# A transformer block on one core: the values' first halves are cast out of PSUM by VectorE instead of ScalarE, with a new order of the work

## The chip, the core and the metric

The kernel runs on one NeuronCore of a Trainium2 chip. Its engines work side by side, each through its own instructions in order: TensorE (PE, matmuls; PEld, its weight loads), VectorE (DVE), ScalarE (ACT), GpSimd (POOL) and SyncE (SP), which issues the DMAs here. The metric is device microseconds for one execution, less being better. The kernel before takes 1051.68 us (median of 3 runs, 1048.98 to 1051.96).

## The reference

The input is x, 8 batches of 512 rows of 512 columns, float32. Cut to what matters:

```python
x = x + layernorm(attention(layernorm(x)))
x = x + layernorm(ffn(layernorm(x)))
# attention: qkv = x @ w_attn + b_attn; 16 heads of 32; a rotation of q and k by head;
#   causal softmax(q k^T) * 512**-0.5 @ v; then @ w_proj + b_proj
# ffn: two layers; each normalises its input, rounds it to 8 bits by the row's largest
#   value, and multiplies by weights rounded to -1, 0, 1 times their mean size;
#   exact gelu between them (512 -> 2048 -> 512)
```

## The kernel before, in words

**Precision.** TensorE multiplies 16-bit floats. Where more is needed, a float32 tile is split in two: a first half, the value rounded to f16, and a remainder, the value minus the first half, also f16. A product then takes three passes (first by first, remainder by first, first by remainder). For the values v the two halves are made out of PSUM at the end of `values` (L538 to L563): the first half by one instruction (L558), the remainder by the next (L560). Both read the same 128x256 float32 piece of an `mm` PSUM tile, and write into one SBUF tile `vt` of 128 x 8 heads x 65 columns: 32 of first halves, a column of ones, 32 of remainders.

**Tiling and streams.** Rows are handled 128 at a time (4 tiles of a batch), heads in groups of 4 (a unit, 128 columns) or in pairs. The work is cut into streams, each a Python generator that yields after every step; a step is a handful of instructions, mostly on one engine. The streams that the text speaks of:

- n, N: load x, normalise it and split it (L491, L496); w, H, J, B, R: load and prepare the attention's weights; t, T, Y: load the feed-forward weights, sum their sizes (L426) and round them (L461)
- Q: queries and keys of a unit (L565; matmuls L575, copies out L587 on ACT and L589 on DVE). V: values of 128 rows and 8 heads (L538): two steps of 6 matmuls (L545), one step with the first half (L558), one with the remainder (L560). There are 64 such pieces
- S: scores (L596; matmuls L610, mask and minimum L624 and L635 on DVE). A: probabilities (L646): exponentials on ACT (L661), a first half on ACT (L667), a remainder on POOL (L669), then DMA transposes `pT<-ph`; 24 steps a unit, 32 units, with transposes in the 12th, 16th, 20th and 24th step. W: the weighted sum of a pair of heads (L682; matmuls L696 of `pT` with `vt`), 7 steps, 64 pairs; the third is the first to read the later transposes
- G, r, P: gather heads, load the residual, project (L741) and add. F, X, Z, C: feed-forward: normalise and quantise (F), expand with Gelu on ACT (X, matmuls L827, Gelu L836; every fifth step), quantise (Z), contract (C, matmuls L883) and store

**The order.** The string `ORDER` (L36 on) holds 4345 letters. The loop at the end of `block_kernel` reads it and takes one step of the named stream for each letter; `pin` (L952) then ties every instruction to the one before it on its engine. So the string fixes the order of the instructions on each engine, the DMA issues on SP included. What it does not fix is time: an engine that waits for another delays what is queued behind.

**Buffers.** PSUM has two `mm` tiles (queries and keys, values, projection, contraction; L120) and three `sc` tiles of two banks (scores, weighted sums, expansion; L119). Matmuls for the next tile of a kind can start only when an older one has been read out.

**Function tables.** ACT loads a function table (ACT_TABLE_LOAD in the trace) when its order goes from an exponential to a Gelu or back.

Of the kernel before, what the change touches and what calls it, by code (L numbers as in the profile page):

```python
# [37 lines left out]
JHJJNNTNRtNtTTtTtTHNNQHQQQQHJnJNtTJHNwYHQYYHYNYQYJQQQHwBYYHQtYYHQJJQHYYQQJSSBTQYYQSQQYYQQHQSSAAQ
AAQVYAAVtVJtYAAAttSSVAQYQAQtQSAAQQQAQJSAAQAABBQQAAAVJSVVAAAQJSAVSVVVVJRVVSAVVVVSAAAVAVnrSVTSQQVA
TVQVAAWNSnQVVQAQWrWWVnWWnQAAAVVTAVQTQQNNNNAWWWWWSWANAWVNNNAAAAAASNNNNNWSSRAATAQAAAASNAWWQNASAANA  # L40
VNVVWWWASGGAAASSWWSWWWWWWAAAAVVVGVAVSVSASNAVVVVAAANAANAWQAAQQQSQSAAAnQGQQGAAWQGSSSQWWWWAAVQAAQVS
WWWWWWWAAVAAAAAQWVAAQRRRRRRQSSAQSSAtWWWQAtASQSQQQAWAQWGGWWWGAVArAWQWQWWWWWASSASAQAVQTQVAATYVQYYY
GGGSSAAAAQQYYYYQQQSQAAAQYAAAPPPPPQPYWPWSSPVPAVPWVVFWWWWPPnAVPASFSFAAAASAAASPVVVAYPYAAAFFQQQQSSQW
WWFWWQWAAAASWAQQAAFAAYQQVSVNNYPSAAANVAVFSYQXAAANNNFAFAAXXXNXNXXAFFXQrnXXGPPFSSNNPPNWGWPVWNNWWAWA
WWVWWWWSPAAAAWVVAAAAVVVASZSYANNNAASFVYVVZArPYYPVAZXWZAAAVFnXXXXXFPXZAAXPXXSSAAAZZZQPGQPQSSWPSQQF
GWZWQQWSWQWAGWAZWWZQWQAWQWCGWZACAQAAQAWSSSAAZAAAQQQQQACAGAAAGASZZCWCWCSAAAVCVVGAAZCSSVQCSCWCWFWQ
WSWQWQAWWWWAAAAACVCWVQQFAAVQSVVZQWVAAASPVVPGQWSZAQQQQFGGNPQAZSSCQAAPQAAQQWWWWNWAAZZXZZVnXWAVANVV
AAAAPSAZXVFFPFZVVPSPNAZZnXASQSWQWWVQWQWAAPWPAZQAAWAQXQQQSQNNCQNSFNXCSAXQAXNnNANAASSFFXPZAXPZZWNr
NANSNNFCWWAWWWCPnGCZGWFPWCPPFWAANWWCZAAANWNWNSPSZZAAAVCVVVCWACAAZACXSCFXVXVXVVPQFSVQSAFFFZVAAAVQ
VZNSFZZXPXAAQQQQXFXQXFAXNQSZPQWPWSPXPWXCCZQWWZZAZZAPCAXFAACQWZPAAZCAPrXCAXZSFZFFZPPCFPSPSCPCXGGC  # L50
XXGWWWWWWGAAXASZZCCACPZWVZANCCCCZrVFCZXSFZVVZWCASQCZWAQAAAAACAQGAAFGSCQQCSCQQWNQWWWZWZZGSAAQCPXA
WQWWWWWWXAPCAAAAACCVSAAQWFZXVVGQVVFSXVSSXVVCrGVZFZXPGVPXSXPFZFFAZAVVQAPQASPAPQAAAAAAAAAWWSQQQQnZ
ZFXXCQCZQAZZCQQCSSCWFWFWWWCAAWWQWWWASCZVWPAVAACWZVSFVQCQnXPZAQFSAXXAZQAAZCZCACCSPASSAPAACASACAZA
XQAAQPXZXPXXPCXPQWWZZFGCZZWQWWQWGXZAZWQXCFAZAXWCWCAWWAWWCPrFNFNXNCQPQVCANAXFZnPFFNXVXNNWSNNAXZZX
ZCCZCSCPNVNCXCPVSSrNZCPnZZZZNCXAXAPZZAZZAFXACAPVNCNNAVSAPSZCXASZCVAVAAAVCZAAZSSAAVVCVSQZPCCASAAA
AXCQCWWSQVCPQVXXWQQWXQWVFVNWQCrPAZQPZZZQPGGGXAPGFZZAQWSQXAQPSCWWAWQWWWACQASNXFACFZZFQCAAASWFCZWW
CAAZAQFQQCGGSXCFQWPWZZZXWWPSAAAAAGAQNFACXACAQAZWSFFFXCSACVWWVnWWWZAAQSQPFXXZZWVXXWAAGVVNXFXSQZAG
FXAQVVSQAGSSZQXXZQCCZVVQZAAAAZQFVQAXSQVVAWFCFFQAZCWZACQAQPCPZXSCSCWPCWPCASXWrAZWZAZZPZZXXZAAAAFA
CWCAAVAACCXCVSnAZSQPPVVrSPPSQCPWWWWWPQPAXAAAQSZZPCAZQFQZZFWCAAZZZSPPQCQCAAAWQFCQCQWCWNNCXWWXWSWG
PAAAAnXQVNGCAFCFFCWWWWWWWNCNNNWAAZVVFXVZAANZZCCNSVAPVSPAVSSVSFrNNAAAAFPAAACPSAAAAANXCNPAXFACXZZn  # L60
CXCXSSXZZNVNZFNCASXAPPCVVZACCAVFFCACCAAXXZZSXSXPFQCCPQrNWWFWAQWPXQXXWXPGGWSZZGQFZZQZZCWWZNXPAAAA
GWPWSAANAAZCZPWWWCAQSCQCQAZAZCQCZSQFAWGQAAZZACQSZQWCCCCQAAWSQQQVXZVSVVQWNWQWPAWQAPVGGQCWAVWWWWWW
XXAnAWSAQQASZSVVXZFGPFXXSQXQGZGCXQFAPAFFAASQASFPZZAAAAQQSAPAFAQAAPZXXQACSAQCSQQQZFFnCSCVWCWVAAZZ
APSWWWWVCFVVrWAWWVCPAZAZZWWAVVVWWAAASFAWnCZZACVCVVSXAAASPZCQFZZZCCXQACAASXAAAQXQQQQSQCSXQWCXCXQN
NXCXCANWCWWCWWZZFSNNNAAACANNAFAAXNNQNNNZQnFFZCVCGCGXWWWXWZWAWWWAFXCCVNFVVVSPNNVPXArZSSSZZAZAVPVS
QNAAAACSAAAAAPZAXXPQXXAQXPPZPPrQQPSQXSPAZQNPPZPZXSQXQFCQXCSAAPXCZZZZSWWCWCWWCAAAAAAFFAZAQAAZQVZC
AVXAZCVVPZAXPXWXPCZCSCFFFXPGGGWWZWPCXWCSWQWFQWFPCAGCAZAQSZSZAWACQZZAQQZCSSFAAACAAAZQNZWPGQCAFrQC
QCSWFQZQZACAVWVVGWWWCVWWWWWVWWCGACAZVAACSWGFVSSVFZVGXVXXVVVGSQXPAAAQPSAAZAVASXXQACrSVVPAQAFQPXFS
AFZAAQAZPXPFQWXZPZQZZNXCPSPPPAAQPQPWnWSWPZnWWQQCPZVCAAWZAAAASAFFFVVnZAVZSCZSCQCQWWQWQCWAWCAASAAA
SAAQQQAAWQCQXQZZNNZXNZCANZZWSXCCNAAACQNCNNCCXASSCWCQVCAZXNNNSCNSNWCWWXCWWCXXAFFAAZAAAGGWWWAWWFNA  # L70
rWNNWSCXAAAXVXWSCCCQXQQFVXZAAZAAQAVSVSSXAZPPFQQFAQSFZZZVAFAAAVXVQXPQXQXPZQQWWPXPZCSCArVPPZXZZZZV
XWWWVVVCVCXAZAXCWPPAZZAPVAVPXCPFZCPFZZZGFGGWSSCPWWWAZCSAAGAZAXPSQSWCQWWZAZZFAQFFFFXCQAXXAAACCWAF
AAACAASCZQCCXXQAZCXZQZACZSrCZQZCQASSWGWCAAWCWWZWACZGXWSCXSQXAAPPZCZCWWWWWWAAAACVAZCSrXZFGAXVQWQX
VXSXAZQCVCSFFFSQAGXPCQCAQCFSFCAZQZQZGZGASQCZAAAAAQCQAWSQQQCXZZFAZZZZAVCXCVVVXWPWAPWAAAAAFPAFWCCP
XPFPXWXVXCPWPFPFXZFZFSXASZCZrZZPVXZPZXPXXAVVACSXAPCSCQZZZZSACWWWWWQCAWAZACAQZFCSPFZPFFFPAFFAXXQW
CCQXQXAZZCCAZZCACWXXCrCZZZPACSWCSZPCPWCSPSCWWCAZZAZPAQAWSQXAZAZFASAAGGWAPPAAFQFXSAPQXCAFFSWWWZXZ
AZAQQPWAPSWWCFCCWPGAAAZAAAAXXPXXSXGAZGPAXAZCFSZZZAPCZSZZVVAFVVAAPAAZZAZACSCCSCGCCCCFAZArWSXZWWWW
WWWWWWWWXWXFSFAFASCASGAACCAPAFFAAAAAAZXAZXXCFXXXXZZZXXXXFCZFFFXZZZCCCGXCXWWCCXCWWWWWWWWWWWWZZGGC
GGZrZZZCXXCCXXZZCPXPZPCPCZPCZPPPCCZZrZFFXXCFFZZZZFXCFZFXCPCCZPCXCXCZZCCPXXZZCPPZPZCPZPFFFXFXPrXP
ZCPCCPPFPPZFZFZPXZZZCFZFXCXXCXXZZZFZCFPCXCCFFPFZCZXXXXZXCPXCCrXPPZZXPPPZZZZXFZZFXCZZFFZZFFFZCXCC  # L80
XCXCXXCZZZZCXXCCCCZCCZCZCXZXZZCCXCXXCXXCZZZZZZZZXZCXXCCZZCXZZXCZZZCZZCCCCCCCCCCZZCCCZZZZZCCZCCCC
# [5 lines left out]
def block_kernel(  # L87
# [450 lines left out]
    def values(b, half, c):  # L538
        xT = xTs[b]
        vt = vts[half * NT + c]  # L540
        ps = mm_tile()
        n = 0
        for hw, hx in PASSES:
            for k in range(NE):
                nc.tensor.matmul(  # L545
                    ps[:, :256],
                    xT[:, c, hx, k, :],
                    wv[hw][:, k, half * 256 : (half + 1) * 256],
                    start=(n == 0),
                    stop=(n == 3 * NE - 1),  # L550
                )
# [6 lines left out]
        nc.scalar.activation(hi, v, AF.Copy, scale=back)  # L558
        yield
        nc.vector.scalar_tensor_tensor(  # L560
            vt[:, :, HD + 1 : 2 * HD + 1], v, back, hi, ALU.mult, ALU.subtract
        )
# [482 lines left out]
```

## Time and profile before

| | |
|---|---|
| median of 3 runs | 1051.68 us (1048.98 to 1051.96) |
| the profiled execution | 1051.51 us |
| its span, first to last instruction | 1049.7 us |
| instructions | 22994 |
| mean granted TensorE clock | 0.978 |
| POOL busy | 759.7 us (72%) |
| DMA, mean | 173 GB/s |
| ACT casts of v, L558 | 64 of 367 to 398 ns, from 64.6 to 906.7 us |
| DVE remainders of v, L560 | 64 of 409 to 425 ns, from 67.4 to 908.1 us |

Times are in microseconds from the span's start. A group of instructions is shown as line, engine, operation, output and inputs, shapes, count, then busy time and the mean of one in ns, then the idle time of that engine just before them and what ended it. A line of the timeline is start, duration, engine, line, operation and count. A row of windows has one engine after another with its busy time and, in brackets, its instructions; after them come the granted TensorE clock (1.00 is full), the mean busy share of the DMA engines (it can pass 1) and GB/s. Matmuls overlap in the pipeline, so PE's busy time and the duration of one matmul overstate what one costs; the distance between starts is the better measure.

### The profile page before, as it was taken

Reading aid. Unit: us, or ns where it says so; the run is one execution under the profiler, and the core shown is the slowest. Engines: PE = TensorE matmul, PEld = TensorE weight load, DVE = VectorE, ACT = ScalarE, POOL = GpSimd, SP = SyncE. Lnnn points to the kernel's source line nnn. Section 1 sums busy time; section 2 is a strip of 40 time slices with the busy share of each in tenths; the row PEclk is TensorE's granted clock in tenths of the full one; section 3 lists DMA queues with packets and bytes.
Section 4 is the critical chain, followed back from the end, with each engine's and each line's share of the span. In section 5 each row is a group of like instructions: output and inputs, shape, how many; then the busy total and the mean of one; then the engine's idle time right before and its main releaser. Section 6 shows DMA issues by size and latency. Waiting matters only on the chain.

```text
span 1049.7 us, 22994 instructions
## 1 busy us (share of the span) xinstructions
PE 977.2 (93%) x8258; PEld 511.0 (49%) x8258; DVE 855.8 (82%) x2674; ACT 904.8 (86%) x1502; POOL 759.7 (72%) x608
## 2 busy tenths in 40 slices
PE   5787888899999999999999999999999999999995
PEld 4544544445555555555545455454454454544442
DVE  7898789989998888887988897888778888866752
ACT  5789998999999998999899999889999889964552
POOL 5249875888877778877888688677967678865544
PEclk9898899999999999999999999999999999999998
DMA  9369998999999988999999999989999879995553
GB/s 308 111 143 205 185 222 128 183 185 194 192 188 181 163 177 163 201 176 183 178 196 177 170 192 178 167 160 192 185 169 175 171 142 170 198 193 110 110 101 80
DMA packets 585027, 181.10 MB, mean 173 GB/s; under 512 B 564304, under 2 KB 568400, under 8 KB 584912
## 3 DMA queue, kind: packets, MB, share of 16 engines
q1 hardware_dynamic: 584912, 179.63, 90.2%
q8 instruction: 64, 1.05, 0.4%
q14 instruction: 51, 0.42, 0.1%
HBM read 29.64 MB, written 8.39 MB: 36 GB/s over the span
## 4 chain that ended last, share of the span: by engine, by line
PE 26%; ACT 25%; DVE 18%; DMA 11%; POOL 10%; issue 9%; SPq 1%; POOLq 0%; ACTq 0%; DVEq 0%
PE sc L827 7%; ACT p L661 6%; PE mm L883 6%; DVE p L624 5%; POOL ph L669 4%; DMA pT<-ph 4%; DMA qT<-q 4%; PE mm L575 4%; ACT ph L667 3%; PE mm L545 2%; PE sc L696 2%; ACT junk L865 2%; ACT h L836 2%; PE mm L741 2%; ACT L836 2%
## 5 line engine op out<-in xcount | busy, mean ns | idle before, releaser
L669 POOL TENSOR_TENSOR ph<-p,ph 128x768 f16<-128x768 f32 (+1 forms) x192 | 355.7, 1856 | 112.8 <-ACT ph L667 92.6
L624 DVE CUSTOM_DVE_ANT_0 p<-sc,mask,e_scale 128x384 f32<-128x384 f32 (+3 forms) x512 | 255.4, 546 | 25.1 <-POOL ph L669 13.2
L883 PE MATMUL mm<-wout,qT 128*128 128x512 fp8e4 x1024 | 260.1, 383 | 6.6 <-ACT row L901 5.1
L827 PE MATMUL sc<-wfc,qT 128*128 128x512 fp8e4 x1024 | 254.6, 379 | 3.9 <-DVE low L624 1.9
L661 ACT ACTIVATE p<-p,nmax 128x384 f32<-128x384 f32 (+3 forms) x512 | 253.5, 552 | 3.0 <-DVE nmax L635 2.5
L575 PE MATMUL mm<-xT,wqk 128*128 128x512 f16 x768 | 203.6, 384 | 2.2 <-DVE vt L560 1.3
L667 ACT CAST ph<-p 128x768 f16<-128x768 f32 (+1 forms) x192 | 172.4, 898 | 5.0 <-DMA pT<-ph 2.0
L827 PEld LDWEIGHTS <-qT 128*128 128x128 f16 x1024 | 96.6, 98 | 117.6 <-issue 9.7
L883 PEld LDWEIGHTS <-qT 128*128 128x128 f16 x1024 | 95.1, 98 | 115.3 <-issue 15.3
L696 PEld LDWEIGHTS <-pT 128*128 128x128 f16 x2560 | 97.1, 98 | 51.6 <-issue 11.9
L575 PEld LDWEIGHTS <-wqk 128*128 128x128 f16 x768 | 70.4, 98 | 83.2 <-issue 16.8
L545 PE MATMUL mm<-wv,xT 128*128 128x256 f16 x768 | 105.1, 278 | 5.8 <-DVE src L589 3.7
L696 PE MATMUL sc<-vt,pT 128*128 128x65 f16 (+1 forms) x2560 | 100.3, 187 | 10.9 <-DMA pT<-ph 4.5
L741 PE MATMUL mm<-wp,oT 128*128 128x512 f16 x384 | 103.2, 381 | 0.8 <-DVE src L589 0.8
L861 POOL TENSOR_SCALAR h<-h,hnm,hqs 128x1024 f32<-128x1024 f32 x64 | 80.1, 1252 | 30.4 <-DVE hnm L857 28.8
L545 PEld LDWEIGHTS <-xT 128*128 128x128 f16 x768 | 73.9, 99 | 37.0 <-issue 11.0
L610 PE MATMUL sc<-src 32*128 32x128 f16 (+3 forms) x1536 | 74.8, 298 | 16.9 <-DVE low L624 9.8
L783 POOL TENSOR_TENSOR q<-h,q 128x1024 f16<-128x1024 f32 x32 | 68.7, 2146 | 24.0 <-ACT q L778 20.1
L865 ACT ACTIVATE junk<-h 128x1024 bf16<-128x1024 f32 x64 | 67.2, 1050 | 16.5 <-DMA qT<-q 12.7
L850 DVE TENSOR_REDUCE htop<-h 128x1 f32<-128x1024 f32 x64 | 76.3, 1211 | 4.6 <-ACT h L836 4.5
L778 ACT CAST q<-h 128x1024 f16<-128x1024 f32 x64 | 66.6, 1040 | 13.2 <-POOL h L861 11.8
L836 ACT ACTIVATE h<-sc,fsc 128x1024 f32<-128x1024 f32 x64 | 71.1, 1111 | 1.9 <-PE sc L827 1.5
(161 smaller groups left out, 1380.8 us busy)
## 6 DMA issues: line engine op xcount, KB each, us to landing
row<-in_x SPq DMA_DIRECT2D x32, 256.0 KB, 3.6
x<-in_x SPq DMA_DIRECT2D x32, 256.0 KB, 3.2
out<-row SPq DMA_DIRECT2D x32, 256.0 KB, 2.7
tw<-in_w_fcT SPq DMA_DIRECT2D x8, 512.0 KB, 8.3
tw<-in_w_outT SPq DMA_DIRECT2D x8, 512.0 KB, 4.4
wraw<-in_w_attn SPq DMA_DIRECT2D x8, 256.0 KB, 4.8
pT<-ph SPq DMA_TRANSPOSE x128, 5.6
qT<-q SPq DMA_TRANSPOSE x96, 4.3
```

Of the source, the lines that this page charges most:

```text
L545: nc.tensor.matmul(ps[:, :256], xT[:, c, hx, k, :], wv[hw][:, k, half * 256 : (half + 1) * 256], start=(n == 0), stop=(n == 3 * NE - 1),)
L575: nc.tensor.matmul(ps, w[:, hw, k, :], xT[:, :, hx, k, :], start=(n == 0), stop=(n == 3 * NE - 1),)
L624: nc.vector.tensor_tensor_reduce(p[:, j, at : at + (i + 1) * P], scs[t][:, j, at : at + (i + 1) * P], mask[:, T - (i + 1) * P :], e_scale[ ...
L661: nc.scalar.activation(pj, pj, AF.Exp, bias=nm[:, i, 2 * t + j : 2 * t + j + 1], scale=-1.0)
L667: nc.scalar.copy(hi, p)
L669: nc.gpsimd.tensor_tensor(lo, p, hi, ALU.subtract)
L696: nc.tensor.matmul(oo[:, j, i, :width], probs[u, PARTS[i]][:, half, j, STARTS[i] + c, :], vt[c][:, h, :width], start=(n == 0), stop=(n == ...
L741: nc.tensor.matmul(ps, oTs[b, k][:, ho, i, :], wp[hw][:, k, :], start=(n == 0), stop=(n == 3 * NE - 1),)
L827: nc.tensor.matmul(ps[:, o1, :], xsT[0][:, n // NE, n % NE, :], wfc[:, n % NE, ts(o, 512)], start=(n == 0), stop=(n == 2 * NE - 1),)
L836: nc.scalar.activation(h[:, ts(o2, 1024)], ps.rearrange("p a f -> p (a f)"), AF.Gelu, scale=xsc, accum_out=hsum[:, o2 : o2 + 1],)
L865: nc.scalar.activation(junk, hh, AF.Square, accum_out=hsq[:, o2 : o2 + 1])
L883: nc.tensor.matmul(ps, hT[0][:, half, k, :], wout[:, o2 * NF // 2 + k, :], start=(n == 0), stop=(n == 2 * NF - 1),)
```

## The change

Of `values`, one line changes; of the order, all but the last line of letters is new:

```diff
         v = ps[:, :256].rearrange("p (h d) -> p h d", d=HD)
         hi = vt[:, :, 0:HD]
         back = 1.0 / (X_S * V_S)
-        nc.scalar.activation(hi, v, AF.Copy, scale=back)
+        nc.vector.tensor_scalar(hi, v, back, None, ALU.mult)
         yield
         nc.vector.scalar_tensor_tensor(
             vt[:, :, HD + 1 : 2 * HD + 1], v, back, hi, ALU.mult, ALU.subtract
```

```diff
 ORDER = """
-nNNNwHIwHHHNwJJNJNNnNHJBBBBBBBBBNNNNRHJJwRRRNNBNBnNHHHNNHHRwJJtHJNNJHRBtnNwwJNJtRHHBBRNNHRNNTJTH
...
+nNwHwHwHJNNNNJBNNtHJnHTJnwNBNBBBBBNBBRHNJRNNRRtBtHNTJHwwNNNHRHHJwJJJnBNHHwNNBNJBRNRJtNtHJHRNwNJB
...
```

Both strings have the same number of letters of each kind. Letters stand at other places throughout, mostly by a few positions: the first t moves from the 63rd letter to the 18th, the first T from the 93rd to the 23rd, I from the 7th to the 154th, the first S from the 171st to the 176th, the first W from the 295th to the 296th, the first X from the 716th to the 725th. The first half's instruction now stands on DVE's queue, after what the order puts before it there; ACT's queue no longer holds it.

More of the change, by code (lines that the diff above doesn't have):

```diff
@@ L36 @@
 ORDER = """
-nNNNwHIwHHHNwJJNJNNnNHJBBBBBBBBBNNNNRHJJwRRRNNBNBnNHHHNNHHRwJJtHJNNJHRBtnNwwJNJtRHHBBRNNHRNNTJTH
[L38 to L81, printed above, removed]
+nNwHwHwHJNNNNJBNNtHJnHTJnwNBNBBBBBNBBRHNJRNNRRtBtHNTJHwwNNNHRHHJwJJJnBNHHwNNBNJBRNRJtNtHJHRNwNJB
+HHHJJNRJRTTHJNNNNNNHnNTJtNtTQtQTTYHHHHQQYQYHYnJNYYtJJYYnJIBYYQQQQQQHHQYYJHQYQTQSSHSYQAQQQYYQQQSS
@@ new lines @@
+QBAAQAYYAAtVAVAAVYVAAASSQQQSQQQSAVAJVAAVJQAVQASAQQAAVStVtQQSABBVAVVVVStVNVSVVJtAArJAAAAAAVTVAAAV
+RAVSSQQWQQVVVWWnWWASAQQQVAVWAQnVTQQTVNNNTNWNNNSSSWNWWWWWWAAAAAAAANNNNSAVSSWATVQWVRAANAASNSNWNNQA
+AAWWWSAAnAAGGWAAASSSVWWWWWAAAGAWVVVSVQQAVNVAAAAWANAASSAAASAQQVVVWASAVGAWRWGSRWAWGAASQAQAQWWQWQWW
+QWWAWAAAAAVQQVQAAARSRRWQVRQVQGSASASSQQrQWQWQWWWWGWAASAAWtWQWWtWNWWSAASAGVVVQAQATTYYVYYSGASGAGAAA
+AAAQYYSAQQQQQQQAYQAYASQPQQYPPWYWPAPYVVVPPSSPPWVPWWAWAWFAASAAPVVArAPSFPWVFSVWWQQAQAASAAAFWQQQFYFW
+QWQSASQWVPAPAQAASVNFNSYAnnPAYAASFVAANAAAQSVAYANNFFNNXGXXAXAAXXXXWAWWWXXWPWPGWQFNANNNNNPPSPSVVWFF
@@ new lines @@
+WWWWWVSAAVAVAVYSASAAAPPVFSAAVYVVYNNZNZYZVAWAAVAAXAXXPAPAAXXPAXPXZrAZPPFXFSSZSXZQQQGZWWWWWFWXGGWQ
+AGQASQQZASSQAQAAWWWWQACWZZQWQWZAACAASSZZSGZZAAAAAGQGCQACSQWQAQAAAAAQZSAACCVWVVSAAVCCCSSQCCSWWWQW
+ZWPAAQFAAWQCWVWVnWWAQWAQAFAVAVAWSVFSQVQVQVGWSACQQZPQNQGGWQSAQnVAQAWWAFPAAASQWVQNXZPWASVPXWFPAXPC
+VSQAPSZAAAVNAQWVWWQAZSZWWNWQVAZZZAZZFAVCXAPAQWQnSrQPFXCSQAXQACQNNXXFNSAFSCNZPNAANQNnQSXNCAWWWWPW
+WPFCPFFAAACAXNPNNNSNGZGWWrCSWWWPVWnZAAAASANWXNAZNAAVAACXXCVVQXPCPZZFWSZFZQZAACAVACAXXQXVVVSXSVQV
+XWWAAZPQVVPQFFQCAZrPFFZFQAFPAWWPXQSWSAPCZPQCFSXAPFQCXPXFQZPZZZXCWAASCZPCAAAAAXSPZFCFFZSZGPZGCGWF
@@ new lines @@
+WXAWWAPVWXVXZAWWAACCAAACZZZSCQCCXZVVCQWZZCWAAQXZZZSQASCWACQQFQGAGPAPCSQCQSWWWZWCZQAAZCSXGWWWWWWF
+XWGNrAAAAAASAXAAACQACAQVAXCACCVWSFVZQVXVQXAGQSSSPQVFFZASGVAXXQNVQVPANCVXnZGPWZVWPVCAAASXNPAWWSCW
+WPZCASQZACAZZQCWAWWWWQWAWAPAZQXZSCXXWPAZFAAQQAAZrAASCXZVCSSCZZZVVASVXXQXQFPFXAAACAACCCPQSPQPFFWA
+PFXFFFSZZAZAQQFQWQPWQCCQNCWCWCXnWANZXZZAZCPPNGXXGZWQAAZCXNCZAWZNCANNQFXFCZSSrNnNZWFnVZNWVCCCPCNC
+ZZWWWWVVXFPXXAXAPASCPNZZZCSZAPXZZCXPCrVSAANNASAAXVCSFVAVCXVZZZNCANAASAAASAZAAPPVZVVZCCCSSQAXAQAC
+WQAPASAAAWACQVCQQWWrWXVXQWXVVPQPQNZFCZPZZQZGGPZGFAXAWSQQAPXCQGSWWAWAQWWWACSAQAXZZCQWWACZFAFWQSQC
@@ new lines @@
+QFCFGFQNSZCAAAXCQFWWWWZZSXXAAACGWSCCGQXZPAFAAZAAAACFSWVWVPWZZAWWWFFSAFQZXQVZVWAXVXPNXSQXZFSGQVXA
+ASXCQVFGCAXZAAQQVXVZSGQQAVQZFZSXVAVQACFFAAQCZWWZCNAAFQQZPCFSAPCAWWPCXSSACPCAPXWZZZZWAZnZnZXXAACC
+AAAAAAWVCSZXVCVSQPPVSSrPCPAAAXAQPWWWWZZPQZCWPPQrAAQZSACFQZZWWFCQAPPACSAAZFSZQCQCQNNCXQFFCWACXXWP
+WWNAGAQNGZNCNNNWWWWWVWAACWCWWVWVXAFAnFnACCAZCrSZNAZVVPVSPSASAANAZVAVPNCSAPAASFNAFNACAAAXXCXXFPCX
+XPNXNNCSCVAAZZSZSCVCZVFXAAACCXZSXPAAAVFQCCAZFZSSPPQPQXXQPGZGNQZXACrGFCXWXWFFFWZZZZQPPZWWWGWWAWCW
+WWXWCAQACNZSCAQCQCZZSZQAAAAACSZZAWAAANQQAACCGCZACCACQWPQSQSWGQCVNQXZQVSQVWQZVWPWQVWWWWQVGPWWWWXX
@@ new lines @@
+WSAAAAAVXZAZZQQSSPFAGXGVGXSQXFFQFrFAAASAAXAQAPAFZQPSASQPQQFPXAQCQSCQCAWWAAAAAAZSXZQCSCZZQVWWVWFP
+WCFAZSVFnVWWFVWWWWWVPAXCAAZZVVVAWCSVSCVVXQXQXZAAAQAAPnnAZAAAZZCCZZCCSSACAZAAFAQQQQXSSQCQCXWAQANC
+NXNCWXNCZXFNCAAWNCANAWWNSAFFFAAXXWCNnNNZGFNGNZZQQVCWWWWWWWXVXCAZNCCWNSPVVVXPNVSZSSCVVPrQAAAPSCZP
+ZAAAAAZAAAAAASZNXXQXXQXPPPPAXQFPSPQQZZZZFSFXQPXXQPCQZSZCSZAAPQCNXAAAAASWWZCWWCAQQVACAVAZAZACArSX
+XWAZZCWZZZVVPPPXXFACCFPFCFXPGGGWWWWWCPGXSWQCWFAAFZZFQPCSCQSZAZCWQACAAAQSCAAAAZAQQWQNCZQCQFQZSZSC
+ZQWZCCVPrNZWGGGAVVVCACWWWFAWWWWWWVWWCVVVVSSAAASAVXVVVXXSVQZXCrCAFPGASAnFFGGPVAQVAAAZFXAXAPASQXQP
@@ new lines @@
+SPAFAAFXQZPSZXZZnQAPSPPPPQPWWQXAPQWWPQZWZAAAWSZPCZQQAZVWFFSFCAVVAAnVCZZZSSCQACAFWQWQWQCWASWAACAA
+AAQSQQZCQZWZAQXQAANNNAXNWZCSNCCAZZASACQANXCCCXCNZQWSNCWVCXZSCWWFANNCNSXCAXWAACAAWNNGrSXGWWAWAWAW
+WWNNANCACAAWXXXCCZVSQVXQZSSAXQAQVXSFAFAAAVQQZFPZSQPZZVCFVVAPQAFAArXXQXFCQPQQXPWPVWPAVZSFZPVVXCVW
+WCWCWZZZZZXXVZXCZZPPAAPVAAVPXPCAZZZFZAAFXPZGGGWSSZSAACPWCWWWWWPAXSQFZFCAZZQSFXFAAAAFCCQXXQAACSAA
+AAACGCCCWFZQQZXZXGZACSAZZASAZCQGCWSQCQCXCWWWWWZWCAAAAAAACCXSAQXSWWZGZCPZCAQXWPWWWZCSXXZVXXWFQFVC
+XVSAQVGACZQrCSSQAXAFZCQAFQPCFZSFAQCQWQWCGQSCQCXZZZAAAAAAFSZQQGVZZXVZCAVVACCrXAWPZAAWPWPWPAFAPACA
@@ new lines @@
+FPFXFZXPZXPPZZZVWXCXFCFSSPXAXAAVPXZPZZVZVSPXZZZZXZZCSQCAQCQAPCQCrSWWPWAWWAASFFAXFFFZFAAQPCFFQZWW
+XACXCCCZZXXCCAACWXZXZZAGZAPWCCSPSCZPSCPZPZZCSrAAAWAWWZSGAWWAAAAAAAFFQCZQCSAQSQQCFXQPFAACPXSPPXZS
+WAACWZWWWAAWZZAAAAZPFXXCFFAXPGWXGAGCAPXPSXXZSZZVZVCVAZSZSAZCAACVASPGrZAAZAZZACPCCCFCFZWWWWWCWWWC
+WWAWXWWXWSXFCSXFSFGPASFAAAAAAAAACCGZFAXZAFAAZXXXCXXXXFCZZZZCXFZFZCFCCWCCWCXXXXGWWWWZXWWWWWWWWZGC
+GXXZZGCCCrCZZXZZZZZXPCCXPPPPPPCrPZZZFFFFCXFXZZZZFZFCCCPZCXCCXCXCCPCXXXZPXZCCZZZPPPZPZCCPFFFFPXPZ
+CPCrPPFPZFFPZPXZZZCXZFZZXCFXPXCXXZZCPZFCXCCCFXFXFPFXZZXXZPCCCrXPZXCZCXPCPPXFZZZZZZXFFFZZZZFFFCZX
@@ L82 @@
+XCCXXXCZCCCCZZZZCZCXXZCZZCCXXZZZZZCCXCXXCZXXCXXXCXXCCCZZZCZZCCCCZZZZZZZCZCCCCCZZZCCCCCCZZZZZCCCC
 CCCCCCCCCCCCCCCCCCCCCCCCC
```

## The prediction

> **What bounds the kernel now.** I read the busy shares first, then the matmuls' own spacing, then busy time by stage, then the waits of the two engines that the edit touches. The first part of the page:
>
> ```profile
> PE 977.2 (93%) x8258; PEld 511.0 (49%) x8258; DVE 855.8 (82%) x2674; ACT 904.8 (86%) x1502; POOL 759.7 (72%) x608
> ```
>
> No engine is the bound by these shares alone: PE is busiest, ACT is 49 us ahead of DVE. Busy PE time is pipelined, so the timeline of PE in a dense stretch gives the real price of a matmul:
>
> ```profile
> 605.72 1.02 PE L883 MATMUL mm<-wout,qT 128*128 128x512 fp8e4 x4
> 606.58 0.82 PE L545 MATMUL mm<-wv,xT 128*128 128x256 f16 x6
> 607.24 0.49 PE L696 MATMUL sc<-vt,pT 128*128 128x65 f16 x12
> 607.57 0.60 PE L545 MATMUL mm<-wv,xT 128*128 128x256 f16 x4
> ```
>
> From start to start, 4 matmuls of 512 columns take 0.86 us (216 ns each), 6 of 256 take 0.66 (110 ns), 12 small ones of L696 0.33 (27.5 ns). Starts of L610's groups lie some 40 ns a matmul apart. The groups of PE between 250 and 900 us hold 2237 matmuls of 512 columns (483 us), 492 of L545 (54), 1754 of L696 (48) and 1044 of L610 (42): 627 of 650 us. So the middle is a dense stream of matmuls, with at most 23 us to win. Busy time by stage:
>
> ```profile
> core 0: us, PE busy (x) PEld busy (x) DVE busy (x) ACT busy (x) POOL busy (x), PEclk, DMA share, GB/s
> 60.00:80.00 20.00, 17.11 (x140) 10.21 (x138) 19.44 (x63) 16.09 (x30) 11.46 (x7) 0.91 0.57 91
> 80.00:150.00 70.00, 55.25 (x681) 33.66 (x683) 56.89 (x202) 66.13 (x121) 60.34 (x45) 0.88 1.09 206
> 150.00:210.00 60.00, 51.82 (x494) 28.04 (x486) 56.26 (x180) 53.19 (x93) 42.65 (x33) 0.97 0.91 160
> ...
> 250.00:900.00 650.00, 641.19 (x5527) 329.11 (x5525) 549.38 (x1711) 609.53 (x990) 505.82 (x394) 1.00 0.97 178
> 900.00:1050.00 150.00, 133.20 (x758) 61.56 (x756) 86.37 (x230) 82.17 (x132) 81.72 (x70) 0.96 0.64 128
> ```
>
> The reader is to see three regimes. Up to about 240 us PE is starved, and DVE is the fullest engine at 60 to 80 (97%) and 150 to 210 (94%), ACT at 80 to 150 (94%). In the middle PE is full and ACT is at 94%. From 900 on the matmuls of the feed-forward part remain. The chain of waits between 130 and 210 us is mostly DVE (26% of it L624 alone); between 400 and 600 it is led by ACT's L661. The edit's two rows, from the groups by form:
>
> ```profile
> L558 ACT ACTIVATE vt<-mm 128x256 f16<-128x256 f32 x64 | 24.5, 382 | 8.5 <-PE mm L545 8.3
> L560 DVE SCALAR_TENSOR_TENSOR vt<-mm,vt 128x256 f16<-128x256 f32 x64 | 26.7, 417 | 12.0 <-ACT vt L558 11.6
> ```
>
> **The change, part by part.** The profiled execution took 1051.51 us (span 1049.7 and 1.8 around it); the runs' median is 1051.68, so the sum holds for both.
>
> *Removed from ACT:* 64 casts of 382 ns, 24.5 us. By windows, 22 of them start before 250 us, 41 between 250 and 900, one after.
>
> *Added to DVE:* 64 TENSOR_SCALAR. The trace has none of this shape. From below, half of L300's (128x512 out of PSUM, 685 ns) is 343 ns; from above, L518's DVE copy of 512 f16 elements out of PSUM takes 418. L560 reads the same 256 PSUM elements and writes the same strided kind of output in 417, so I take 417: 26.7 us, bounds 22 and 27. The second instruction reads what the first wrote; dependent pairs such as L767 and L768 show about 35 ns of idle, 64 of them 2 us.
>
> The Trainium skill, "ScalarE: Activation LUTs", section Rules for kernel authors, tells the author to use VectorE rather than ScalarE for plain multiplications, up to about 3 times faster in bf16. The rows here disagree for fp32 out of PSUM: DVE's 417 is slower than ACT's 382. By the rule an added cast would be an estimated 127 ns, 8 us in all, and the start-up term below would vanish.
>
> *Start-up, to 250 us.* DVE gets 22 x 0.417 = 9.2 us. In the 80 to 150 window it idles 13 us, which hides the 9 casts there (4 + 9 + 6 + 1 of the 22 lie in 60:80, 80:150, 150:210, 210:240). In the two full windows the 10 casts cost 4.2. In four places before 250 us DVE stood idle for the ACT cast (4.4 us in all; ACT itself waited 4.4 for PE there, so that PE wait stays and DVE now does the cast where it idled): 4 x 0.417 = 1.7 comes back. Ten dependent gaps cost 0.3. Net 2.8, **+3**. Bounds: 0, if DVE's 30 us of idle to 250 hide everything, and 10 (9.2 and 22 gaps of 35 ns). What waits behind the cast on DVE is mainly L624, which frees the score tiles; PE waited 9.8 us for "DVE low L624" in nine places, so that is where a later DVE shows.
>
> *Middle.* ACT loses 41 x 0.382 = 15.7. But the new order alternates more often between the exponentials (steps A) and the Gelus (every fifth X step). Each alternation reloads the function table: the trace has 36 loads at L836 and 35 at L661, 1283 ns each, and counting alternations along the old order gives the same 71. The new order has 77, all six more in the middle: 6 x 1.283 = 7.7. ACT ends 8 us lighter (601 of 650). PE's waits that name ACT's h, row or p sum to only 2.4 us there, so I take **-2**; bounds 0 and -8. DVE's 17.1 more (566 of 650) lies beside full PE; without that cover it would cost up to 17.
>
> *The order itself.* I counted, in both orders, how much matmul work (steps times the spacings above) stands between the step that issues a unit's last transposes of probabilities (20th and 24th A step) and the W step that first reads them. Over 64 pairs of heads the mean falls from 10.2 to 8.9 us, and the leads under 5 us rise from 7 to 15. These transposes take 5.6 us from issue to landing (median). The same count falls for the first half of a unit (14.6 to 14.0), for F to X (15.5 to 14.2) and for Z to C (15.6 to 14.9), and rises a little for inputs to V (15.5 to 15.9). PE waited 6 times, 4.5 us, for "DMA pT<-ph". Eight more short leads at 0.75 each are 6.0; ACT being lighter brings the transposes forward, so I take **+4**; bounds 0 and 8 x 1.9 (the longest such wait) = 15. The early weight loads (t from the 63rd step to the 18th, T from the 93rd to the 23rd) move past the N loads on SP's queue and to ACT time that is free: ACT is busy 32 of the first 50 us. I take 0 for it, with 3 us either way (T's 1.25 us twice, or one 512 KB load in the way).
>
> The row at 100 to 110 us has PE busy 5.44 of 10 and a granted clock of 0.67, 3.3 us of lost clock. The Trainium skill, "TensorE: Matmul & The Clock Gate", section HAM oscillation, says a PE gap past about 3.4 us brings half clock. If the new leads made such gaps, each would add an estimated 1.7 us; waits as short as those counted would add none.
>
> Sum: 1051.5 + 3 - 2 + 4 = 1056.5; I say **1056**.
>
> **The rivals.**
>
> *ACT is the middle's bound (faster).* For it: ACT is 94% busy at 250 to 900 and leads the chain at 400 to 600. Against: PE is 96.5% full by spacing. Its price: all 8 us of ACT's relief, and 1.7 in the start-up with the DVE term hidden: 1051.5 - 8 - 1.7 = 1042. It decides as soon as a lighter ACT starts exponentials early enough that PE's 23 us of gaps shrink by more than the order's short leads add.
>
> *PE's density decides (no change).* The start-up's 9.2 us go into DVE's 30 us of idle, short leads are covered by the lighter ACT, and the matmul stream after 240 us is the same work: 1051.5, give or take 3.
>
> *DVE carries the whole bill (much slower).* All 9.2 + 0.8 us of the start-up and the 6.0 of short leads: 1051.5 + 16 = 1067. For it: DVE leads the chain at 130 to 210. Against: its idle at 80 to 150.
>
> That the cast doesn't move can't be: the diff names the engine.
>
> **How the numbers follow.** A measurement of this kernel tells about 0.3% (3.2 us) from no change. Chances: forecast (1055 to 1062) 0.37, whole bill (above 1062) 0.10, no change 0.23, ACT bound 0.30. So faster 0.30, same 0.23, slower 0.47. Both signs hold weight, so the range reaches from the ACT rival's 1042, less 1, to just under the whole bill, 1066; the forecast's own range is 1053 to 1062.
>
> **What would show it.** Right: DVE's group at L558 near 417 ns, DVE near 883 us busy and ACT near 888; 77 or 78 table loads; more PE waits on pT than 6; DVE fuller than 94% at 150 to 210 with PE waiting longer for L624. Wrong: PE idle falling in 250 to 900, or the start-up (time at which the 50 us windows reach 48 of PE) coming earlier. A cast much under 343 ns would undo the start-up term; unchanged waits on pT would undo the order's.

## The result, and the profile after

The changed kernel takes 1062.35 us (median of 6 runs, 1057.94 to 1065.49) where the kernel before takes 1050.53 beside it (6 runs, 1048.98 to 1052.73): a ratio of 1.011, with a 95% interval of 1.0092 to 1.0128, or 11.8 us slower. The profiled execution took 1062.45 us (span 1060.7, mean granted clock 0.974 where it was 0.978). The forecast was 1056.

The first part of the page and the two rows of the edit, all of the changed kernel:

```profile
PE 982.6 (93%) x8258; PEld 512.7 (48%) x8258; DVE 875.0 (82%) x2738; ACT 899.3 (85%) x1444; POOL 757.2 (71%) x608
```

```profile
L558 DVE TENSOR_SCALAR vt<-mm 128x256 f16<-128x256 f32 x64 | 26.8, 419 | 9.9 <-PE mm L545 8.7 <-PE sc L696 1.1
...
L560 DVE SCALAR_TENSOR_TENSOR vt<-mm,vt 128x256 f16<-128x256 f32 x64 | 26.9, 421 | 1.4
```

The work moved as it should: 64 casts more on DVE, at 419 ns against the 417 taken. DVE's wait for ACT's cast (11.6 us before) is gone and DVE now waits for the matmuls of `values` itself, 8.7 us, where ACT waited 8.3. Summed over engines, DVE gained 19.2 us and ACT lost 5.5. No engine is fuller than 93%, as before, and yet the kernel is 1.1% longer. So the shares don't tell where the time went. Windows do; these are the stages of the prediction, in the changed kernel (core's microseconds, then PE, PEld, DVE, ACT, POOL busy, clock, DMA):

```profile
60.00:80.00 20.00, 18.86 (x158) 12.07 (x157) 19.55 (x66) 17.46 (x31) 12.90 (x8) 0.93 0.54 91
80.00:150.00 70.00, 50.85 (x638) 30.72 (x635) 57.78 (x197) 58.07 (x99) 56.01 (x42) 0.83 1.08 214
150.00:210.00 60.00, 53.76 (x500) 28.97 (x501) 56.03 (x186) 54.18 (x92) 44.00 (x34) 0.94 0.89 157
...
250.00:900.00 650.00, 633.33 (x5433) 324.32 (x5432) 558.43 (x1729) 597.85 (x940) 496.63 (x388) 1.00 0.97 175
900.00:1062.00 162.00, 145.72 (x870) 67.47 (x868) 97.08 (x262) 94.05 (x150) 92.56 (x77) 0.96 0.68 134
```

The reader is to see the matmul count of the middle: 5433 where the kernel before had 5527 in the same 650 us. The middle isn't only lighter on ACT (597.85 of 650 where it was 609.53), it gets less work through, and the matmuls that are missing there stand behind 900 us (870 where there were 758). Splitting the middle shows that the loss lies in its first third. The kernel before, then the changed kernel:

```profile
250.00:450.00 200.00, 197.89 (x1708) 102.48 (x1705) 172.88 (x533) 189.13 (x308) 158.12 (x127) 1.00 0.99 182
450.00:900.00 450.00, 443.30 (x3821) 226.63 (x3820) 376.50 (x1179) 420.40 (x683) 347.70 (x268) 1.00 0.96 176
```

```profile
250.00:450.00 200.00, 190.18 (x1625) 98.19 (x1624) 168.61 (x528) 184.35 (x288) 153.13 (x122) 0.99 0.95 174
450.00:900.00 450.00, 443.15 (x3809) 226.13 (x3808) 389.83 (x1202) 413.49 (x653) 343.49 (x267) 1.00 0.97 176
```

PE is 7.7 us less busy between 250 and 450 and the same, to 0.15 us, between 450 and 900. Counting the matmuls that have started by a given time, each once and at the spacings of the prediction (216 ns for 512 columns and so on), gives the same account in finer steps; the text calls this matmul work. The work that the changed kernel is behind by is 1.8 us at 250 us of its span, 8.3 at 350, 11.9 at 450, 13.1 at 600 and 12.2 at 900. It loses about 2 us in the start-up, about 10 between 250 and 450, and nothing after that.

### The profile page after: what moved, and what is told of

Its sections match the earlier page's. It is cut to its first block, busy times and chain, and to the rows that moved or that the text cites. A ratio compares the mean times of both kernels' runs of the same rounds, so it can differ in the third digit from the quotient of the medians.

```text
span 1060.7 us, 22988 instructions
## 1 busy us (share of the span) xinstructions
PE 982.6 (93%) x8258; PEld 512.7 (48%) x8258; DVE 875.0 (82%) x2738; ACT 899.3 (85%) x1444; POOL 757.2 (71%) x608
## 5 line engine op out<-in xcount | busy, mean ns | idle before, releaser
L669 POOL TENSOR_TENSOR ph<-p,ph 128x768 f16<-128x768 f32 (+1 forms) x192 | 354.6, 1849 | 114.4 <-ACT ph L667 93.1
L545 PE MATMUL mm<-wv,xT 128*128 128x256 f16 x768 | 104.6, 277 | 5.3 <-DVE src L589 2.7
L741 PE MATMUL mm<-wp,oT 128*128 128x512 f16 x384 | 104.0, 382 | 1.7 <-DMA oT<-hT 1.0
L783 POOL TENSOR_TENSOR q<-h,q 128x1024 f16<-128x1024 f32 x32 | 68.8, 2151 | 31.0 <-ACT q L778 30.7
L545 PEld LDWEIGHTS <-xT 128*128 128x128 f16 x768 | 73.3, 99 | 34.8 <-issue 9.3
L865 ACT ACTIVATE junk<-h 128x1024 bf16<-128x1024 f32 x64 | 67.2, 1050 | 11.2 <-DMA qT<-q 10.5
```

Of the source, the lines that this page charges most:

```text
L545: nc.tensor.matmul(ps[:, :256], xT[:, c, hx, k, :], wv[hw][:, k, half * 256 : (half + 1) * 256], start=(n == 0), stop=(n == 3 * NE - 1),)
L669: nc.gpsimd.tensor_tensor(lo, p, hi, ALU.subtract)
L741: nc.tensor.matmul(ps, oTs[b, k][:, ho, i, :], wp[hw][:, k, :], start=(n == 0), stop=(n == 3 * NE - 1),)
```

## The experiments

Each kernel was timed beside the kernel before on the same chip, and the groups ran on different chips, so times are compared as ratios to the kernel before. In microseconds, 1.0100 is 10.5. E1 to E4 part the edit from the order, F and G the cast from what the cast costs, I the function tables, J and K the fit of the orders.

### Order alone, cast alone

e1 is the kernel before with the new ORDER and the cast left on ScalarE; e2 is the kernel before, its order untouched, with the one line of the cast:

```diff
-        nc.scalar.activation(hi, v, AF.Copy, scale=back)
+        nc.vector.tensor_scalar(hi, v, back, None, ALU.mult)
```

> The new order with the cast left on ScalarE. Theory ORDER (the new order costs the time, by its tighter leads and six more table loads, whoever casts): slower than before by 9 to 16 us, since ScalarE now has the 24.5 us of casts and 7.7 us more of table loads, 617 of 650 us in the middle. Theory CAST (VectorE's 26.7 us more costs the time, and the order was made to soften it): within 4 us of before. Theory BOTH (the order fits only the cast on VectorE): slower than the changed kernel, by over 4 us, that is over 16 us above before.

> The old order with the cast on VectorE. Theory ORDER: within 4 us of before (the start-up term of the prediction, +3, less what the lighter ScalarE gives, 2 to 8). Theory CAST: slower than before by 9 to 16 us, as much as or more than the changed kernel. Theory BOTH: slower by 4 to 9 us, since the old order isn't made for the cast on VectorE.

Measured: e1 1110.59 us, ratio 1.0584 (1.0558 to 1.0611); e2 1072.32 us, 1.0222 (1.0199 to 1.0244). Each half alone is worse than both together. With the old order the move of the cast costs 22 us; with the new order it wins 48 (60 less 12). Neither ORDER nor CAST explains that, since each would have left one of the two kernels near the kernel before. BOTH stands, each order being fitted to the engine that its casts run on, though not in its sizes: e2 was put at 4 to 9 us above the kernel before and is 22.

How a wrong fit looks is seen in the waits of ACT (what waited, for whom, microseconds in all, times, longest), first in the kernel before, then in e1:

```profile
ACT vt L558 <- PE mm L545: 8.3, 9, 2.2
```

```profile
ACT vt L558 <- PE mm L545: 50.3, 29, 4.6
```

The new order puts the cast where DVE can wait for the matmuls of `values`. The same place in ACT's queue holds the exponentials up behind it: 42 us more of waiting in one line, 29 times. Part of e1's loss is TensorE's clock: the mean granted clock is 0.964 in e1's profiled execution and 0.975 to 0.985 in the kernel before's runs beside it.

### The start alone, the rest alone

The casts are on VectorE in both. e3 has the first 960 letters of the new order (about the first 240 us), and behind them the letters that are left in the old sequence; e4 has the first 960 of the old order, and the rest in the new sequence. The two starts hold the same letters but for three.

> The cast on VectorE; the new order for the first 960 letters (to about 250 us), then the old order for what is left. In the trace of the changed kernel its matmul work is 3 us behind before's at 250 us and 13 behind at 900. Theory ORDER, with most of the loss in the middle: slower than before by 0 to 5 us. Theory CAST: slower by 9 to 16, as with any order. If the start-up sets the loss by leaving the later work out of step: also 9 to 16, with the old table loads (72) back.

> The cast on VectorE; the old order for the first 960 letters, then the new order for what is left. Theory ORDER, with the loss in the middle: slower than before by 7 to 14 us, with 78 table loads. Theory CAST: 9 to 16 and the same as with the old order throughout. If the new start-up sets the loss: within 4 us of before.

Measured: e3 1069.13 us, 1.0174 (1.0147 to 1.02); e4 1069.85 us, 1.0186 (1.0162 to 1.021). A new start under the old rest wins only 3 of the 22 us of e2 by the medians, 5 by the ratios, whose intervals just touch, and an old start under the new rest costs 8 more than the changed kernel. By matmul work, e4 is 8.3 us behind at 250 us, where the changed kernel is 1.8. So the new start is worth some 6 us to a VectorE cast. From 250 to 450 e4 loses another 8.2, much like the changed kernel's 10.1: that loss belongs to the new rest, whatever stands in front of it.

### What a cast on DVE costs in the old order

f1 leaves the cast on ScalarE and adds, in the same step, one independent VectorE instruction over 256 elements (it measured 409 ns):

```diff
         nc.scalar.activation(hi, v, AF.Copy, scale=back)
+        nc.vector.tensor_reduce(extra, ones[:, None, :].to_broadcast([P, 2, P]), AX.XY, ALU.max)
         yield
```

> The kernel before, its cast left on ScalarE, with one more VectorE instruction in each of the 64 cast steps: a reduction of 128x256 constants that waits for nothing and that nothing waits for (about 0.41 us, 26 us in all). Theory TIME (VectorE's own time is what costs: it delays what is queued behind it, PE loses that and, being full, never wins it back): slower by 14 to 26 us, as the cast on VectorE in the old order is (+22). Theory PLACE (VectorE standing still for the values' matmuls is what costs): within 4 us. Theory FIT (any shift between engines breaks the order): slower by 5 to 20, and leaving work out is slower too.

Measured: 1057.65 us, 1.0079 (1.0057 to 1.01). That is in FIT's range and below TIME's. DVE's time by itself is worth some 8 of e2's 22 us; 5 of the 8 are lost before 250 us, by matmul work.

f5 issues the VectorE cast a step later, in the step of the remainder, so that DVE has not to stand before the matmuls are through:

```diff
-        nc.scalar.activation(hi, v, AF.Copy, scale=back)
         yield
+        nc.vector.tensor_scalar(hi, v, back, None, ALU.mult)
         nc.vector.scalar_tensor_tensor(
```

> The old order, the cast on VectorE but issued in the remainder's step, right before the remainder, so that VectorE stands for the values no earlier than it does in the kernel before. Theory PLACE: most of the 22 us of the cast at ScalarE's place goes; 5 to 12 above before (what an idle 0.41 us on VectorE cost). Theory TIME: 18 to 24 above before, the place being of no matter.

Measured: 1069.46 us, 1.0204 (1.0191 to 1.0218), where e2 has 1.0222. DVE's wait for L545 did fall, from 12.0 us in e2 to 4.2, and the time didn't follow. PLACE falls: DVE standing early before the matmuls isn't what costs. The number is in TIME's range, but f1 has put DVE's time at 8 us.

### Casts left out or cut short

f2 and g1 leave the cast out of the old order, g3 out of the new one; f3 and g2 (old order) and f4 (new order) cast one head of eight on VectorE, 32 columns, 182 ns. The tiles' unwritten parts are filled with 1.0 beforehand, in f2 to f4 at the start, where that fill set PE back by about 2 us by 50 us in f2 and f3 (not in f4), and in g1 to g3 at the end of the weight loads:

```diff
-        nc.scalar.activation(hi, v, AF.Copy, scale=back)
+        nc.vector.tensor_scalar(hi[:, 0:1], v[:, 0:1], back, None, ALU.mult)
```

```diff
         wraws[s, g] = w
+        if (s, g) == (1, NG - 1):
+            for t in vts:
+                nc.gpsimd.memset(t, 1.0)
         yield
```

> The old order with the cast left out: vt is filled with 1.0 at the start instead of the first halves being written, so the values are not the reference's; the remainder stays on VectorE and waits for PE alone. ScalarE does 24.5 us less. Theory TIME: 0 to 8 us faster than before, the prediction's worth of a lighter ScalarE. Theory PLACE: the same. Theory FIT: slower by 3 us or more although work is taken away.

> The old order, the cast on VectorE at its place but of one head's 32 columns only (the other first halves are left at 1.0, filled at the start): the same wait for PE, about 0.19 us instead of 0.42, 12 us in all. Theory TIME: half the cost of the whole cast, 8 to 13 us slower than before. Theory PLACE: the whole cost, 18 to 24 slower. Theory FIT: anything between 5 and 22.

> The new order (changed kernel) with the cast cut to one head's 32 columns, the others left at 1.0: VectorE does 14.6 us less than in the changed kernel. Theory TIME: 6 to 12 us faster than the changed kernel, so 0 to 6 above before. Theory PLACE: like the changed kernel, 10 to 13 above before. Theory FIT: not faster than the changed kernel, perhaps slower, as the order expects the longer cast.

> As the old order with the cast left out (the first halves are 1.0), but vt is filled by GpSimd some 40 us later, where it has nothing to do: the fill at the start had put the matmuls 2.3 us back by 50 us. Theory FIT (less work on ScalarE makes the old order slower all the same): 3 to 7 us above before. Otherwise, the 7 us having been the fill: 3 below to 2 above before; a lighter ScalarE is then worth at most 3 us.

> The old order, the cast on VectorE at ScalarE's place, one head's 32 columns only, with the late fill. Theory PLACE: 14 to 22 above before, close to the whole cast (22). Theory TIME: 6 to 12 above, in proportion to 0.19 of 0.42 us.

> The new order with the cast left out altogether (first halves 1.0, late fill), 72 to 78 table loads as in the changed kernel. Theory ORDER (the new order is itself the slower one, by its short leads and table loads): 7 to 13 above before, like the changed kernel. Theory PLACE or TIME (the cast on VectorE is the cost, the order having made up for part of it): 4 below to 4 above before.

| the cast | old order | new order |
|---|---|---|
| on ScalarE | the kernel before, 1 | e1 1.0584 |
| none, fill at the start | f2 1.0072 (1.0044 to 1.01) | |
| none, late fill | g1 1.0056 (1.0043 to 1.0069) | g3 1.0153 (1.013 to 1.0176) |
| one head of eight on VectorE, fill at the start | f3 1.0181 (1.0146 to 1.0215) | f4 1.0131 (1.0107 to 1.0155) |
| the same, late fill | g2 1.0167 (1.0139 to 1.0195) | |
| all on VectorE | e2 1.0222 (1.0199 to 1.0244) | the changed kernel 1.011 (1.0092 to 1.0128) |

Two things are to be read here. In the right column the new order is slower than the kernel before by 12 to 16 us whether the cast on VectorE is whole, short or not there at all; its own price isn't that cast. In the left column, less work is slower: the old order without any cast is 0.56% longer than with the cast that it was written for. f3 and g2 (19 and 17 us) lie in PLACE's ranges and above TIME's: a cast of 0.18 us costs nearly what one of 0.42 does, and the 15 us that DVE saves bring 4 to 6. Since f5 speaks against PLACE, neither theory covers the old order; FIT, which names no mechanism, is what is left. The groups of DVE may hold a part of the reason. Five of its lines (L465, L469, L761, L783, L785) work on tiles in SBUF and are stretched where they meet an instruction of POOL. Above their usual durations they take 20.0 us too long in the kernel before, 21.1 in f1, and 26.9 to 28.7 in f3, g1, g2 and e2: 7 to 9 us more when ACT's casts are gone from the old order, most of it before 250 us. But e3, with the new start, is 18 us slower with 21.5 us of it, and i1 (below) is no slower with 24.6. No experiment took these collisions away by themselves, so how much of the time they make is not shown. In the new order they are no more than before (18.1 in the changed kernel, 20.8 in g3).

### Without the function tables

i1 is the kernel before and i2 the changed kernel with the Gelu computed as an exponential, so that ACT keeps one table:

```diff
-                AF.Gelu,
+                AF.Exp,
```

> The kernel before with the Gelu replaced by the exponential (other values come out), so that ScalarE never switches tables: some 71 loads of 1.28 us go, 91 us of ScalarE. If ScalarE sets the middle's pace: 10 us or more faster than before, up to the 23 us of PE's gaps. If PE does: within 4 us, or slower where earlier ScalarE work shifts VectorE and GpSimd against each other.

> The changed kernel with the Gelu replaced in the same way: 77 loads go. Theory LOADS (the new order's loss is its six more table loads): the 12 us shrink to 4 or less against the old order without table switches. Theory SPACING (its loss is where steps stand against what they wait for): 8 us or more above the old order without table switches.

Measured: i1 1052.71 us, 1.0018 (1.0001 to 1.0036); i2 1058.16 us, 1.0069 (1.0046 to 1.0091). The first part of the page, i1 and then i2:

```profile
PE 976.4 (93%) x8258; PEld 511.0 (49%) x8258; DVE 859.6 (82%) x2674; ACT 813.4 (77%) x1431; POOL 759.1 (72%) x608
```

```profile
PE 979.6 (93%) x8258; PEld 511.6 (48%) x8258; DVE 879.9 (83%) x2738; ACT 798.7 (76%) x1367; POOL 758.6 (72%) x608
```

ACT goes from 904.8 to 813.4 us in the old order, and the kernel gains nothing; its matmul work stays within 1.3 us of the kernel before's from 50 to 900 us. ACT is therefore not the bound there, and an ACT that is lighter by the 24 us of the casts had nothing to give. In the new order the relief of all 77 loads brings 4 us (1.011 to 1.0069); the two intervals lie side by side. i2 is then 5 us slower than i1, between the 4 or less of LOADS and the 8 or more of SPACING: the loads are a part of the new order's loss, and not the larger one.

### How much one letter is worth

j1 (kernel before) and j2 (changed kernel) swap 252 pairs of neighbouring letters, one of the feed-forward part (X, Z, C) and one of another stream, drawn by chance, one draw for each kernel. That moves steps by one place and adds no work, but for six more switches of the table in j2 (83 where the new order has 77; j1 keeps the old order's 71):

> The kernel before, the cast on ScalarE, with 252 of the 878 places where a step of the attention stands next to a step of the feed-forward part (X, Z, C) swapped by chance; every step moves by one place at most and the table switches stay 71. Theory TUNED (the old order is fast by its exact sequence): 5 to 15 us slower. Theory ROBUST (orders differ only by what they do on a large scale): within 4 us.

> The changed kernel with as many neighbours swapped in the same way (82 or 83 table switches, up to 8 us more of ScalarE). Theory TUNED for the old order alone: within 6 us of the changed kernel, either way, since the new order has little to lose. If the new order is as finely fitted as the old: 5 to 15 us slower than the changed kernel.

Measured: j1 1070.95 us, 1.0193 (1.0172 to 1.0214); j2 1086.9 us, 1.0349 (1.0326 to 1.0372), 25 us above the changed kernel. A shift of one place for 504 of 4345 letters costs nearly as much as the whole move of the cast in e2 (20 and 22 us); a letter stands for 0.24 us on average. The new order is fitted as finely as the old, and both cost more than TUNED had said (5 to 15); ROBUST falls.

### The short leads, lengthened

The prediction had counted short leads. k1 takes the changed kernel and issues 13 loads of the residual earlier; k2 takes the late steps of the weighted sum of 19 pairs of heads later. Both are edits of ORDER alone; one line of k1's is

```diff
-VSQAPSZAAAVNAQWVWWQAZSZWWNWQVAZZZAZZFAVCXAPAQWQnSrQPFXCSQAXQACQNNXXFNSAFSCNZPNAANQNnQSXNCAWWWWPW
+VSQAPSZAAAVNAQWVWrWQAZSZWWNWQVAZZZAZZFAVCXAPAQWQnSQPFXCSQAXQACQNNXXFNSAFSCNZPNAANQNnQSXNCAWWWWPW
```

> The changed kernel, its order altered in 13 letters only: the loads of the residual (r) that the new order issues less than 10 us of matmul work ahead of the projection's last step are issued earlier, so that each has about 12 us (the five shortest had 0.0, 1.7, 1.8, 2.1 and 3.0). Nothing else moves. LOADS (short leads of loads are a part of the new order's cost): the PE gap of 2.04 us near 282 us, behind which VectorE waited 0.98 us for a load of the residual, goes, and the time falls by 2 to 5 us, to 1057 to 1060. SPREAD (the cost lies in the fit as a whole, and such a gap only shows it): the time stays within 2 us of the changed kernel's 1062.35, whatever becomes of that gap.

> The changed kernel, its order altered only in the weighted sums (W) of 19 pairs of heads: their steps from the third on, which first read the late transposes of probabilities, are taken 1 to 30 letters later, as far as the score tiles allow. The leads under 5 us fall from 15 to 8 of 64 pairs (the old order has 7), the mean rises from 8.9 to 9.4 us. LEADS (the term as the prediction priced it, 0.75 us for each of eight short leads, was too small because each costs more, and 12 us stand for the eight): the time falls by 6 to 10 us, to 1052 to 1056. SPREAD: the leads of the transposes are not what costs; the time stays within 3 us of 1062.35, or rises, since 19 moved groups disturb other queues (252 single swaps cost 25 us, which makes 1 to 3 for these).

In k2 two of the 64 pairs (the 4th and the 36th) read one of their four value tiles only after it has been rewritten for the next batch; the amount of work is the same.

Measured: k1 1064.09 us, 1.0133 (1.0105 to 1.0162); k2 1067.56 us, 1.0169 (1.0142 to 1.0197). Neither brought the time down. SPREAD stands, and what LOADS and LEADS forecast didn't come, though k2 moved much besides the leads. k1 shows in one place why an earlier load didn't help. In the changed kernel PE stands for 2.05 us at 282 us, for DVE. Its timeline, and beside it g3's, whose lines are numbered two higher and which has no cast at all:

```profile
280.77 1.03 PE L883 MATMUL mm<-wout,qT 128*128 128x512 fp8e4 x4
283.84 0.87 PE L696 MATMUL sc<-vt,pT 128*128 128x65 f16 x26 [2.05 <-DVE low L624]
284.56 1.31 PE L741 MATMUL mm<-wp,oT 128*128 128x512 f16 x3
285.67 0.79 PE L696 MATMUL sc<-vt,pT 128*128 128x65 f16 x14
286.30 1.45 PE L741 MATMUL mm<-wp,oT 128*128 128x512 f16 x3
287.53 1.33 PE L883 MATMUL mm<-wout,qT 128*128 128x512 fp8e4 x4
288.70 0.81 PE L741 MATMUL mm<-wp,oT 128*128 128x512 f16 x3
```

```profile
279.62 1.03 PE L885 MATMUL mm<-wout,qT 128*128 128x512 fp8e4 x4
282.69 1.14 PE L698 MATMUL sc<-vt,pT 128*128 128x65 f16 x26 [2.04 <-DVE low L626]
```

The gap costs more than its 2.05 us. When PE runs again, the three matmuls of L741 last 1.31 and 1.45 us, where from 288.70 on they last 0.81: the granted clock is 0.50 for the 3.4 us from 284.7 on, which is 1.7 us lost. The same gap, of 2.04 or 2.05 us, and the same 3.4 us at 0.50 behind it are in e1, f4, g3, j2, k1 and k2; i2 has the gap and keeps its clock. The kernel before has neither, as the clock of this stage shows (third number from the end; the kernel before, then the changed kernel):

```profile
250.00:350.00 100.00, 98.83 (x892) 51.86 (x890) 87.23 (x274) 95.20 (x158) 81.47 (x67) 1.00 1.00 182
```

```profile
250.00:350.00 100.00, 93.62 (x817) 48.02 (x816) 84.14 (x268) 91.59 (x147) 74.86 (x60) 0.98 0.98 175
```

Ahead of the gap, in the changed kernel, DVE's L761 waits for a load that was issued late. So the load looks guilty. POOL and DVE there:

```profile
278.32 2.12 POOL L669 TENSOR_TENSOR ph<-p,ph 128x1024 f16<-128x1024 f32 x1
```

```profile
279.35 1.64 DVE L761 SCALAR_TENSOR_TENSOR x<-row,pr,x 128x512 f32<-128x512 f32 x1 [0.98 <-DMA x<-in_x]
```

In k1 the load is there in time, and the wait is gone:

```profile
278.97 2.12 POOL L669 TENSOR_TENSOR ph<-p,ph 128x1024 f16<-128x1024 f32 x1
```

```profile
278.95 2.70 DVE L761 SCALAR_TENSOR_TENSOR x<-row,pr,x 128x512 f32<-128x512 f32 x1
```

```profile
284.50 0.68 PE L696 MATMUL sc<-vt,pT 128*128 128x65 f16 x19 [2.05 <-DVE low L624]
```

L761 now takes 2.70 us instead of 1.64 (usually 0.75). It ends 0.56 us after POOL's instruction (281.65 against 281.09), much as in the changed kernel (280.99 against 280.44). The gap on PE is 2.05 us again. By the trace, what sets it is that POOL's L669 and L761 meet at this place of the order, and the wait for the load only lay inside that time; no run takes the collision alone away.

In k2 the leads are longer and the wait for the transposes is longer too. Here are the kernel before, the changed kernel and k2:

```profile
PE sc L696 <- DMA pT<-ph: 4.5, 6, 1.9
```

```profile
PE sc L696 <- DMA pT<-ph: 5.8, 8, 1.6
```

```profile
PE sc L696 <- DMA pT<-ph: 10.5, 7, 3.8
```

Of k2's 10.5 us, 3.84 fall at 125 us, where the changed kernel waited 1.61. By matmul work k2 is 3.9 us behind the changed kernel at 250 us already and 8.7 at 700 (its profiled execution took 1073.08 us).

## Why the prediction was wrong

The direction was right: slower. The size wasn't: 12 us and not 4.5. Point by point:

**The step that failed is the last term, "the order itself", taken as +4 with bounds 0 and 15.** It measured about 12: with the cast on VectorE whole, cut to one head or left out, the new order is 12 to 16 us slower than the kernel before (the changed kernel, f4, g3). I had put a price of 0.75 us on each of eight more short leads of the transposes. That was the wrong thing to count. PE's waits on `pT` rose from 4.5 us to 5.8, by 1.3 and not by 6, and k2, which takes the count from 15 short leads back to 8, is 5 us slower and not 6 to 10 faster. The cost of this order isn't the sum over its short leads. The changed kernel's gaps of over 0.4 us between 245 and 460 add up to 8.1 us (1.9 before), and they stand behind different resources: the score tiles that DVE has to free, and the transposes `oT`, `pT` and `qT`. The 6.2 us more and the 1.7 of half clock behind the gap at 282 us make 8 of the 10 us lost there. The prediction had let waits as short as these cost no clock, and this one did. The gap at 282 us recurs in g3 (2.04 us), and that at 438 us, of 1.19 us, in g3 (1.18) and in e4, here:

```profile
442.24 0.34 PE L610 MATMUL sc<-src 32*128 32x384 f16 x2
443.76 0.66 PE L610 MATMUL sc<-src 32*128 32x384 f16 x10 [1.19 <-DVE low L624]
```

With PE 96.5% full, nothing after 450 us wins such a gap back.

**Middle, -2, should have been close to 0.** It rested on a lighter ACT. i1 takes 91 us from ACT in the old order and the time doesn't fall; all 77 loads are worth 4 us in the new one (i2). The count of table loads behind the term was right: the 77 alternations shown here, and one first load at L241, make 78.

```profile
L836 ACT ACT_TABLE_LOAD x39 | 50.0, 1283 | 2.0 <-DVE wout L469 1.2 <-DVE htop L854 0.2
...
L661 ACT ACT_TABLE_LOAD x38 | 48.8, 1283 | 0.6
```

**Start-up, +3: the number nearly met, the cause mostly not.** The changed kernel is 1.8 us behind at 250 us, but g3, without any cast, is 1.0 behind there. Less than 1 us is left for 22 casts, which were priced at 2.8; in the old start they weren't hidden so (e4 is 8.3 behind, g1 without a cast 4.5). The granted clock was lower too (0.83 for 0.88 at 80 to 150, 0.94 for 0.97 at 150 to 210); what that cost isn't told apart.

**The price of one cast was right:** 417 ns taken, a median of 417 and a mean of 419 measured. The Trainium skill's rule for plain multiplications ("ScalarE: Activation LUTs", Rules for kernel authors) would have made it an estimated 127; fp32 out of PSUM doesn't show that.

**The signs.** PE did wait more often for `pT` (8 times, 6 before), and the table loads came as counted. DVE didn't get fuller at 150 to 210 (56.03 us, 56.26 before), which already spoke against the start-up term. PE's idle time between 250 and 900 us rose, from 8.8 us to 16.7, so that sign of being wrong stayed away. DVE ended at 875 busy where 883 was forecast, and ACT at 899 where 888 was. There the prediction's sums were at fault. ACT's instructions lasted in all 24.5 us less for the casts and 7.7 more for the loads, as counted; but neighbouring instructions overlap in the trace, and busy time counts an overlap once. The 64 casts alone held only 13.7 us of ACT's busy time before, and hold 20.6 of DVE's after: 904.8 - 13.7 + 7.7 is 899, and 855.8 + 20.6 is 876.

**The rivals.** "ACT is the middle's bound" falls by i1 for the old order. "PE's density decides" was right that a full PE hides the busy time of the others (f1's 26 us of extra DVE work cost 8, 5 of them before 250 us), and wrong that it hides a new order: j1 adds no work and costs 20. "DVE carries the whole bill", at 1067, is nearer to the measured 1062.35 than the forecast's 1056 is, by luck and not for its reason: it put 10 us on the start-up, which lost 1.8, and 6 on the short leads.

**What stays open.** Why this new order is a poorer fit than the old one was for its own cast, and whether another order for the VectorE cast could reach 1050 us. About 4 of its 12 us go with the table loads (i2), of which up to 1.7 may be the half clock that i2's profiled execution doesn't have, and the rest is spread over gaps that the two trials k1 and k2 didn't remove. In the old order, 8 of e2's 22 us are DVE time (f1) and 5 come with ACT's queue running without the cast (g1), if the two add; the 9 that are left were not told apart.
